# A graph, attention and mixture-of-experts block on one core: both layers' weight product moved to the front, the routing in 16-bit floats, the gates carried in the gathered rows

## The chip, the core and the metric

The kernel runs on one core of a Trainium2 chip. The metric is the device time of one execution in microseconds (us); a lower time is better. The profile is one execution taken with the hardware profiler; its times are counted from the first instruction, and its span from the first to the last.

The engines are named as in the profile: PE is TensorE's matmul, PEld its weight load, DVE is VectorE, ACT is ScalarE, POOL is GpSimd, SP is SyncE, which computes nothing and issues DMAs. Every engine takes its instructions in the order of the program; L405 is line 405 of the kernel. ACT and POOL can issue DMAs too.

## The reference

All data is 32-bit float. There are N = 1250 nodes with D = 768 features and 41,250 edges given as lists `src` and `dst` sorted by `dst`.

```python
xn = layernorm(x)
# graph part: two layers of attention over the edges, heads 4 x 192, then 2 x 96
h    = (layernorm(xn) * g + b) @ W1
e    = leaky_relu(s_src[src] + s_dst[dst])        # s = (h * a).sum(-1) per head
out1 = segment_sum(softmax over dst(e) * h[src], dst) + b1
out2 = the same with W2, a_src2, a_dst2, b2 on out1
gnn  = concat([xn, out2]) @ Wu + bu
# linear attention: q, k = elu(xn @ W + b) + 1, 12 heads of 64
mix  = (q @ (k.T @ v)) / (q @ k.sum) @ Wo + bo
x    = x + gnn + mix
# mixture of experts: 8 experts of 768 -> 384 -> 768, the best 2 for each node
xl   = layernorm(x); gate = xl @ Wg + bg
x    = x + sum over the best 2 experts e of gate[e] * (gelu(xl @ fW1[e] + fb1[e]) @ fW2[e] + fb2[e])
```

## The kernel before

Nodes are worked on in ten tiles of 125 (`NT = 10`). A tile framework takes the Python program, gives every instruction a place on its engine by priorities and its own model of durations, and sets the semaphores. So an instruction may stand far from its line's neighbours; the order on each engine is fixed when the program is built.

**Counting.** Edges are turned into a dense matrix of counts `AT` (125 partitions x 10 x 1250). A short start loads the edge lists, sorts out keys, and tests in a branch (L240) whether the slow general way is needed; it isn't for this data. Then `chunk` runs 41 times: two one-hot compares on DVE (`l_hot`, `k_hot`, L335), eight matmuls (`ec`, L350) and four additions into `AT` on DVE (L356). Between the chunks of each tile stands `features(t)`: the layer norm of a tile (L307 to L311) and six transposes (L319) with their copies (L321) into `xnT`.

**The weight product.** `weights()` folds layer 2 into layer 1. It makes the columns `W2e` from `W2` and the attention vectors (a product L381 and a reduction L383 for each of the two vectors), transposes `W1` in 48 matmuls (L394, copies L396), multiplies it with `W2e` (L405), scales the result into `Wg1` (L410), and makes two constant rows (L398, L417, L420, copied by L422 and L423). In the program it stands after tile 1. `gathered(t)` (L430) then multiplies each tile by `Wg1`; the framework puts these matmuls between the later chunks. When the memory of `weights()` is free, the loads of `Wk` and `Wv` (L453 to L455) follow on SP's queue.

After the last chunk the mask is made (L461 transposed by L465), and six heads of attention run (L504 to L569), with the k and v projections (L607) between them.

**Mix and routing.** For each tile: the q projection (L751), the sum over all parts (L781, L792), a layer norm, the row `xl` written to a table in HBM (`xl_d`, L802), the gate (L807, L810), and the routing. The routing ranks the eight gates (L817 to L826), counts places with two small matmuls (`pp`, L830), splits each place into a slot and a row, and writes two values into `inv`, the node's number and its gate, by matmuls of one-hots (`hot`, `put`, L849 to L854). All of it is in 32-bit floats. After the last tile `idx` (node of every place) and `gs` (gate of every place) are read out of `inv`.

**Experts.** Each expert has three fixed groups of 128 places. `gather(e)` fetches three groups of rows by indirect DMAs on POOL's queue (`xg`, L909; three buffers), and transposes them (L912). `hidden` and `give` are the two layers (L926, L938). `give` adds the bias, multiplies by the gate (L942), and adds the result to the output by an indirect, accumulating DMA on POOL's queue (L943). The program's order is

```python
xT = gather([r for r, _ in fixed(0)])
for e in range(NE):
    hT = hidden(ring[e], xT, FIX, fb1T[:, :, e:e + 1])
    if e + 1 < NE:
        xT = gather([r for r, _ in fixed(e + 1)])
    for j, (rows, gates) in enumerate(fixed(e)):
        give(ring[e], hT, j, rows, gates)
    if e + 4 < NE:
        ring.append(expert(fW1[e + 4], fW2[e + 4], fb2[e + 4]))
```

`expert` loads weights (L656 and L658, 1.15 MB each, and the bias L661) into a ring of four. Accumulating DMAs into the output wait for each other. After the eight experts, `other` treats one more group whose expert is known at run time only, and further ones under branches that this data doesn't take.

Of the kernel before, what the change touches and what calls it, by code (L numbers as in the profile page):

```python
# [38 lines left out]
N, D = 1250, 768  # L39
# [30 lines left out]
def gps_block(ctx: ExitStack, tc: tile.TileContext, x, src, dst, norm_g, norm_b, W1, a_src1, a_dst1,  # L70
# [60 lines left out]
    xl_d = dram.tile([N + 128, D], F32)  # L131
# [18 lines left out]
    def load_tile(t):  # L150
        xts[t] = ln.tile([PT, D], F32, name="xt", bufs=2)
        for p, tt in token_rows(t):
            nc.sync.dma_start(xts[t][p], xr[p, tt])

    load_tile(0)
# [4 lines left out]
    nb_row = fl.tile([96, D], F32)  # L160
    nc.sync.dma_start(W1_sb, W1.rearrange("(c p) f -> p c f", p=128))
# [6 lines left out]
    for t, a in zip(a2, (a_src2, a_dst2)):  # L168
        nc.sync.dma_start(t.rearrange("p h c -> p (h c)"), row_bcast(a, 96))
    nc.sync.dma_start(nb_row, row_bcast(norm_b, 96))  # L170

    rows = fl.tile([KC, 128], F32)
    colv = const.tile([128, KC], F32)
    nc.sync.dma_start(rows, norm_g.rearrange("(c p) -> c p", p=128))
    rows96 = fl.tile([26, 96], F32)
    col96 = const.tile([96, 26], F32)
    nc.sync.dma_start(rows96[0:8], b1.rearrange("(c p) -> c p", p=96))
    nc.sync.dma_start(rows96[8:10], b2.rearrange("(c p) -> c p", p=96))
    for k, a in enumerate((a_src1, a_dst1)):
        nc.sync.dma_start(rows96[10 + 8 * k:18 + 8 * k], a.rearrange("h (c p) -> (h c) p", p=96))  # L180
# [145 lines left out]
    with tc.tile_pool(name="ma_p", bufs=2, space=PSUM) as ma_p:  # L326
# [44 lines left out]
        def weights():  # L371
# [6 lines left out]
            for k in range(2):  # L378
                pr = fw.tile([96, 2, D], F32, name="W1T", bufs=2).rearrange(
                    "p a (i h c) -> p (a i) h c", h=H2, c=C2)  # L380
                nc.vector.tensor_mul(pr, heads2, a2[k][:, None].to_broadcast([96, 8, H2, C2]))  # L381
                at = 2 * (C2 + 1) + 2 * k
                nc.vector.tensor_reduce(W2e[:, :, at:at + 2], pr, AX.X, ALU.add)  # L383
# [54 lines left out]
        with tc.tile_pool(name="hot", bufs=2) as hot, \  # L438
                tc.tile_pool(name="ec_p", bufs=2, space=PSUM) as ec_p:
            for t in range(NT):  # L440
                for i in range(t * NC // NT, (t + 1) * NC // NT):
                    chunk(i, hot, ec_p)
                features(t)
                if t == 1:
                    weights()
                    setup.close()
                    kp = kps.enter_context(tc.tile_pool(name="kp", bufs=1, side="right"))
                    Wk_sb = kp.tile([128, KC, D], F32)
                    Wv_sb = kp.tile([128, KC, D], F32)
# [236 lines left out]
    zero = fp.tile([128, D], F32)  # L686
    nc.gpsimd.memset(zero, 0.0)
    nc.sync.dma_start(xl_d[N:], zero)
    nc.sync.dma_start(out[N:], zero)
# [4 lines left out]
    gs = fp.tile([128, NV + 1], F32)  # L694
# [4 lines left out]
    with ExitStack() as rs:  # L699
# [7 lines left out]
        def numbers(shape, pattern, base, mult, name):  # L707
            t = rp.tile(shape, F32, name=name)
# [8 lines left out]
        row128 = numbers([PT, 128], [[1, 128]], 0, 0, "row128")  # L717
        steps = numbers([128, NE, NJ - FIX], [[0, NE], [128, NJ - FIX]], 128 * FIX, 0, "steps")
        slot_row = numbers([PT, NV], [[1, NV]], 0, 0, "slot_row")
# [13 lines left out]
        nc.gpsimd.memset(gs[:, NV:], 0.0)  # L733
# [34 lines left out]
        for t in range(NT):  # L768
# [30 lines left out]
            xl = rl.tile([PT, D], F32, name="xl")  # L799
            normalise(xl, xt)  # L800
            for p, tt in token_rows(t):
                nc.sync.dma_start(xlr[p, tt], xl[p])  # L802
# [20 lines left out]
            sel = rl.tile([PT, NE], F32, name="sel")  # L823
# [13 lines left out]
            both = rl.tile([PT, 2, 2], F32, name="both")  # L837
            nc.vector.tensor_reduce(both, two, AX.X, ALU.add)
            b_i = rl.tile([PT, 2], I32, name="b_i")
            nc.vector.tensor_copy(b_i, both[:, 0])  # L840
# [6 lines left out]
            for k in range(2):  # L847
                hot = rl.tile([PT, 128], F32, name="hot")
                nc.vector.tensor_scalar(hot, row128, s_f[:, 1, k:k + 1], None, op0=ALU.is_equal)  # L849
                put = rl.tile([PT, 2, NV], F32, name="put")  # L850
                for i, v in enumerate((node1[:, t:t + 1], both[:, 1, k:k + 1])):
                    nc.vector.tensor_scalar(put[:, i], slot_row, s_f[:, 0, k:k + 1], v,
                                            op0=ALU.is_equal, op1=ALU.mult)
                nc.tensor.matmul(inv.rearrange("p a s -> p (a s)"), hot,  # L854
                                 put.rearrange("p a s -> p (a s)"), start=k == 0 and t == 0,
                                 stop=k == 1 and t == NT - 1)
        free = rp.tile([128, NV], F32)
        nc.vector.tensor_scalar(free, inv[:, 0], 0.0, nobody, op0=ALU.is_equal, op1=ALU.mult)
        nc.vector.scalar_tensor_tensor(idx[:, :NV], inv[:, 0], -1.0, free, op0=ALU.add,
                                       op1=ALU.add)  # L860
        nc.vector.tensor_copy(gs[:, :NV], inv[:, 1])
# [42 lines left out]
    def gather(rows):  # L904

        xT = sp.tile([128, KC, FIX * 128], F32, name="xsT")
        for j, r in enumerate(rows):
            xg = sp.tile([128, D], F32, name="xg", bufs=3)
            nc.gpsimd.indirect_dma_start(xg, None, xl_d, bass.IndirectOffsetOnAxis(r, 0))  # L909
            px = x_p.tile([128, 2, 512], F32, name="px")  # L910
            for c in range(KC):
                nc.tensor.transpose(px[:, c // 3, (c % 3) * 128:(c % 3 + 1) * 128],  # L912
                                    xg[:, c * 128:(c + 1) * 128], ident)
# [3 lines left out]
        return xT  # L917

    def hidden(w, xT, n, bias):
# [11 lines left out]
    def give(w, hT, j, rows, gates):  # L931
# [9 lines left out]
        nc.vector.tensor_add(halves(ys), py[:, :, :384], halves(wb))  # L941
        nc.scalar.mul(ys, ys, gates)  # L942
# [3 lines left out]
    def fixed(e):  # L946
        return [(idx[:, v:v + 1], gs[:, v:v + 1]) for v in range(e * NJ, e * NJ + FIX)]

    xT = gather([r for r, _ in fixed(0)])
    for e in range(NE):  # L950
        hT = hidden(ring[e], xT, FIX, fb1T[:, :, e:e + 1])
        if e + 1 < NE:
            xT = gather([r for r, _ in fixed(e + 1)])
        for j, (rows, gates) in enumerate(fixed(e)):
            give(ring[e], hT, j, rows, gates)
        if e + 4 < NE:
            ring.append(expert(fW1[e + 4], fW2[e + 4], fb2[e + 4]))

    def other(k):
# [7 lines left out]
        gates = sp.tile([128, 1], F32, name="gates")  # L967
        nc.vector.tensor_copy(gates, gs[:, bass.ds(ve, 1)])
# [4 lines left out]
        hT = hidden(w, gather([rows]), 1, bias)  # L973
        give(w, hT, 0, rows, gates)
# [41 lines left out]
```

## Time and profile before

| | us |
|---|---|
| median of 3 runs | 1179.41 (1175.86 to 1180.65) |
| the profiled execution | 1180.66 |
| its span | 1178.6 |
| PE busy | 1077.8 (91%) |
| DVE busy | 669.1 (57%) |
| ACT busy | 358.1 (30%) |
| POOL busy | 76.3 (6%) |

The profiled execution spends 2.1 us outside its span and stands 1.25 us above the median. Stages, by the first and last instructions of their lines: the start to 20.3, counting with the weight product to 193, the mask to about 212, attention to 594, loads and the k/v product to 622, mix and routing to about 937, experts to the end. A busy PE says only that matmuls are in its pipe; where it is the engine that others wait for must be read from the chain of waits and the timeline.

### The profile page before, as it was taken

How to read it: one execution, taken by the hardware profiler on the slowest of the kernel's cores; microseconds unless marked ns; L12 is line 12 of the kernel's file. 1: busy time of each engine (PE TensorE's matmuls, PEld its weight loads, DVE VectorE, ACT ScalarE, POOL GpSimd, SP SyncE). 2: the span in 40 equal slices, each digit the busy share in tenths (PEclk: the TensorE clock that was granted, in tenths of full speed). 3: DMA queues.
4: the chain of work that ended last, by engine and by line, in shares of the span. 5: the costliest groups of instructions: out<-in, count | busy, mean ns of one | idle time of the engine just before them, and what ended most of it. 6: DMA issues, size and time to landing. Idle time of an engine off the chain costs nothing.

```text
span 1178.6 us, 12106 instructions
## 1 busy us (share of the span) xinstructions
PE 1077.8 (91%) x4583; PEld 723.6 (61%) x4583; DVE 669.1 (57%) x1366; ACT 358.1 (30%) x527; POOL 76.3 (6%) x100
## 2 busy tenths in 40 slices
PE   2599998999999999988989999999999589999993
PEld 2586655578788878544545666666666356666652
DVE  6866666669696966687922555555555422222210
ACT  2131114373737373373712211111111011111111
POOL 1000000000000000000000000000000122322321
PEclk9999998999999999989989999999999789999997
DMA  5014000000000001000083111111123537777533
GB/s 156 27 51 163 16 25 1 1 1 1 1 1 1 1 1 53 1 0 1 1 319 103 40 40 40 40 40 40 39 65 106 191 91 188 200 209 219 121 56 54
DMA packets 33282, 79.62 MB, mean 68 GB/s; under 512 B 5258, under 2 KB 13020, under 8 KB 33208
## 3 DMA queue, kind: packets, MB, share of 16 engines
q1 hardware_dynamic: 27608, 59.02, 15.2%
q0 software_dynamic: 5600, 19.66, 8.4%
q8 instruction: 40, 0.66, 0.2%
q14 instruction: 34, 0.28, 0.1%
HBM read 60.37 MB, written 18.30 MB: 67 GB/s over the span
## 4 chain that ended last, share of the span: by engine, by line
PE 70%; DVE 20%; DMA 5%; issue 2%; ACT 2%; POOL 1%; DVEq 0%; SPq 0%; POOLq 0%; ACTq 0%
PE po L781 13%; PE ph L926 8%; PE py L938 7%; PE mm L430 7%; PE mm L607 7%; PE mm L751 7%; DVE scr L515 6%; DVE w L535 5%; DVE w L536 5%; PE ag L548 3%; PE ag L569 2%; PE u L792 2%; PE px L912 2%; PE mm L405 2%; DMA w<-in_L_gnn_Wu_dram 2%
## 5 line engine op out<-in xcount | busy, mean ns | idle before, releaser
L548 PE MATMUL ag<-kept,w 125*125 125x198 f32 x800 | 137.4, 333 | 5.1 <-DVE w L536 4.9
L548 PEld LDWEIGHTS ag<-kept,w 125*125 125x125 f32 x800 | 133.5, 188 | 9.0 <-DVE w L536 9.0
L926 PE MATMUL ph<-xsT,w 128*128 128x384 f32 (+1 forms) x324 | 100.6, 470 | 1.8 <-DVE xsT L915 1.8
L938 PE MATMUL py<-w,hT 128*128 128x384 f32 x300 | 100.6, 486 | 0.0
L430 PE MATMUL mm<-Wg,xnT 128*125 128x400 f32 x240 | 91.8, 520 | 1.0 <-DVE xnT L321 0.6
L607 PE MATMUL mm<-Wv_sb,xnT 128*125 128x384 f32 x240 | 85.7, 489 | 4.8 <-DVE kvacc L627 4.8
L535 DVE TENSOR_TENSOR w<-v,w 125x1250 f32<-125x1250 f32 x60 | 86.3, 1453 | 6.6 <-ACT w L533 5.9
L515 DVE CUSTOM_DVE_ANT_0 scr<-ss_row,mask 125x1250 bf16<-125x1250 f32 x60 | 87.2, 1453 | 0.5 <-ACT ss_row L506 0.2
L781 PE MATMUL po<-w,xnT 128*125 128x384 f32 x240 | 84.8, 496 | 2.6 <-DMA w<-in_L_gnn_Wu_dram 2.6
L536 DVE SCALAR_TENSOR_TENSOR w<-w,AT 125x1250 f32<-125x1250 f32 x60 | 86.4, 1455 | 0.4
L926 PEld LDWEIGHTS ph<-xsT,w 128*128 128x128 f32 x324 | 59.8, 193 | 41.4 <-DVE xsT L915 2.4
L607 PE MATMUL mm<-Wk_sb,xnT 128*125 128x384 f32 x240 | 84.4, 486 | 0.0
L534 ACT ACTIVATE v<-dn_row,sl 125x1250 f32<-125x1250 f32 x60 | 79.3, 1333 | 16.9 <-DVE w L535 16.4
L751 PE MATMUL mm<-w,xnT 128*125 128x384 f32 x240 | 84.2, 489 | 0.0
L915 DVE COPY xsT<-px 128x384 f32<-128x384 f32 x50 | 25.5, 552 | 99.2 <-PE px L912 77.3
L781 PE MATMUL po<-w,qT 128*125 128x384 f32 x240 | 80.8, 486 | 0.0
L938 PEld LDWEIGHTS py<-w,hT 128*128 128x128 f32 x300 | 55.3, 190 | 33.9
L941 DVE TENSOR_TENSOR ys<-py,wb 128x768 f32<-128x768 f32 x25 | 23.9, 958 | 74.0 <-PE py L938 45.5
L781 PEld LDWEIGHTS po<-w,xnT 128*125 128x125 f32 x240 | 44.2, 190 | 30.1 <-DMA w<-in_L_gnn_Wu_dram 2.8
L781 PEld LDWEIGHTS po<-w,qT 128*125 128x125 f32 x240 | 44.2, 188 | 29.4
L607 PEld LDWEIGHTS mm<-Wv_sb,xnT 128*125 128x125 f32 x240 | 42.4, 187 | 31.1 <-DVE kvacc L627 6.9
L751 PEld LDWEIGHTS mm<-w,xnT 128*125 128x125 f32 x240 | 43.6, 188 | 27.6 <-ACT qT L321 0.2
(274 smaller groups left out, 1415.6 us busy)
## 6 DMA issues: line engine op xcount, KB each, us to landing
w<-in_L_ffn_W_dram SPq DMA_DIRECT2D x18, 1152.0 KB
xt<-in_x_dram SPq DMA_DIRECT2D x20, 336.0 KB
wb<-in_L_ffn_b_dram SPq DMA_DIRECT2D x9, 384.0 KB
out_dram<-xt SPq DMA_DIRECT2D x10, 336.0 KB
xl_d<-xl SPq DMA_DIRECT2D x10, 336.0 KB
W_sb<-in_L_gnn_W_dram SPq DMA_DIRECT2D x1, 2304.0 KB
Wk_sb<-in_L_mix_Wk_dram SPq DMA_DIRECT2D x1, 2304.0 KB
Wv_sb<-in_L_mix_Wv_dram SPq DMA_DIRECT2D x1, 2304.0 KB
```

Source lines behind the costliest of these rows:

```text
L430: nc.tensor.matmul(ps[:PT, :2 * (CG + 2)], xnT[:, c, t * PT:(t + 1) * PT], Wg1[:, c, 2 * k:2 * k + 2].rearrange("p h c -> p (h c)"), start ...
L515: nc.vector.tensor_tensor_reduce(scr, ss_row, mask[:, t], 1.0, 0.0, ALU.mult, ALU.max, top[:, t:t + 1])
L534: nc.scalar.activation(v, dn_row, AF.Exp, bias=sl[:, st:st + 1])
L535: nc.vector.tensor_tensor(w, v, w, op=ALU.max)
L536: nc.vector.scalar_tensor_tensor(w, w, 2.0, AT[:, st, :N], op0=ALU.min, op1=ALU.mult)
L548: nc.tensor.matmul(ag[:, t // 2, o:o + CG], w[:, t * PT:(t + 1) * PT], gw[:, st, hd], start=st == 0 and t % 2 == 0, stop=st == NT - 1, ski ...
L607: nc.tensor.matmul(ps[:PT, :384], xnT[:, c, t * PT:(t + 1) * PT], w[:, c, half], start=c == 0, stop=c == KC - 1)
L751: nc.tensor.matmul(ps[:PT, :384], xnT[:, c, tk], Wq_sb[:, c, half], start=c == 0, stop=c == KC - 1)
L781: nc.tensor.matmul(po[k][:, :384], l, r[:, k * 384:(k + 1) * 384], start=i == 0, stop=i == len(parts) - 1)
L915: nc.vector.tensor_copy(xT[:, 3 * a:3 * a + 3, j * 128:(j + 1) * 128], px[:, a, :384].rearrange("p (b n) -> p b n", b=3))
L926: nc.tensor.matmul(ph[:, :n * 128], w[0][:, o:o + 128], xT[:, c, :n * 128], start=c == 0, stop=c == KC - 1)
L938: nc.tensor.matmul(py[:, k, :384], hT[:, f, j * 128:(j + 1) * 128], w[:, o:o + 384], start=f == 0, stop=f == FC - 1)
```

## The change

`weights()` is called before the first tile's chunks. Its eight small loads are issued by ACT instead of SP and stand ahead of the others in the program; the first tile of `x` is loaded after `W1` and `W2`. `pr` gets memory of its own. The loads of `Wk` and `Wv` stand after tile 2 instead of tile 4.

In the routing, `row128`, `slot_row`, `ones`, `tri`, `cum`, `sel`, `hot` and `put` become 16-bit floats, and `inv` holds only the node's number. The gate leaves the routing: it is written into eight further columns of the row table `xl_d` (776 columns instead of 768), comes back with the gathered row `xg`, and `give` reads it there. So `xg` is kept until its `give` is done, and has six buffers instead of three. `hidden` is renamed `inner`.

```diff
-    xl_d = dram.tile([N + 128, D], F32)
+    xl_d = dram.tile([N + 128, D + NE], F32)
...
-    load_tile(0)
     W1_sb = fl.tile([128, KC, D], F32)
...
+    nc.scalar.dma_start(rows, norm_g.rearrange("(c p) -> c p", p=128))
...
+    nc.scalar.dma_start(rows96[0:8], b1.rearrange("(c p) -> c p", p=96))
+    nc.scalar.dma_start(rows96[8:10], b2.rearrange("(c p) -> c p", p=96))
+    for k, a in enumerate((a_src1, a_dst1)):
+        nc.scalar.dma_start(rows96[10 + 8 * k:18 + 8 * k], a.rearrange("h (c p) -> (h c) p", p=96))
     nc.sync.dma_start(W1_sb, W1.rearrange("(c p) f -> p c f", p=128))
...
     for t, a in zip(a2, (a_src2, a_dst2)):
-        nc.sync.dma_start(t.rearrange("p h c -> p (h c)"), row_bcast(a, 96))
-    nc.sync.dma_start(nb_row, row_bcast(norm_b, 96))
...
+        nc.scalar.dma_start(t.rearrange("p h c -> p (h c)"), row_bcast(a, 96))
+    nc.scalar.dma_start(nb_row, row_bcast(norm_b, 96))
+    load_tile(0)
     load_tile(1)
...
-                pr = fw.tile([96, 2, D], F32, name="W1T", bufs=2).rearrange(
+                pr = fw.tile([96, 2, D], F32, name="pr").rearrange(
...
+            weights()
             for t in range(NT):
                 for i in range(t * NC // NT, (t + 1) * NC // NT):
                     chunk(i, hot, ec_p)
                 features(t)
-                if t == 1:
-                    weights()
+                if t == 0:
                     setup.close()
...
-                if t == 4:
+                if t == 2:
                     nc.sync.dma_start(Wk_sb, Wk.rearrange("(c p) f -> p c f", p=128))
...
-        ones = rp.tile([PT, 128], F32)
+        ones = rp.tile([PT, 128], F16)
-        tri = rp.tile([PT, 128], F32)
+        tri = rp.tile([PT, 128], F16)
-        cum = rp.tile([PT, NT + 1, NE], F32)
+        cum = rp.tile([PT, NT + 1, NE], F16)
-        inv = g_p.tile([128, 2, NV], F32, name="inv", bufs=1)
+        inv = g_p.tile([128, NV], F32, name="inv", bufs=1)
...
-            xl = rl.tile([PT, D], F32, name="xl")
-            normalise(xl, xt)
+            xl = rl.tile([PT, D + NE], F32, name="xl")
+            normalise(xl[:, :D], xt)
...
-            gate = rl.tile([PT, NE], F32, name="gate")
+            gate = xl[:, D:]
             nc.vector.tensor_add(gate, pg[:PT, :NE], bg_b)
+            for p, tt in token_rows(t):
+                nc.sync.dma_start(xlr[p, tt, D:], gate[p])
...
-            two = rl.tile([PT, 2, 2, NE], F32, name="two")
-            for i, a in enumerate((at, gate)):
-                nc.vector.tensor_mul(two[:, i], kth, a[:, None, :].to_broadcast([PT, 2, NE]))
+            two = rl.tile([PT, 2, NE], F32, name="two")
+            nc.vector.tensor_mul(two, kth, at[:, None, :].to_broadcast([PT, 2, NE]))
...
-                hot = rl.tile([PT, 128], F32, name="hot")
+                hot = rl.tile([PT, 128], F16, name="hot")
                 nc.vector.tensor_scalar(hot, row128, s_f[:, 1, k:k + 1], None, op0=ALU.is_equal)
-                put = rl.tile([PT, 2, NV], F32, name="put")
-                for i, v in enumerate((node1[:, t:t + 1], both[:, 1, k:k + 1])):
-                    nc.vector.tensor_scalar(put[:, i], slot_row, s_f[:, 0, k:k + 1], v,
-                                            op0=ALU.is_equal, op1=ALU.mult)
-                nc.tensor.matmul(inv.rearrange("p a s -> p (a s)"), hot,
-                                 put.rearrange("p a s -> p (a s)"), start=k == 0 and t == 0,
+                put = rl.tile([PT, NV], F16, name="put")
+                nc.vector.tensor_scalar(put, slot_row, s_f[:, 0, k:k + 1], node1[:, t:t + 1],
+                                        op0=ALU.is_equal, op1=ALU.mult)
+                nc.tensor.matmul(inv, hot, put, start=k == 0 and t == 0,
                                  stop=k == 1 and t == NT - 1)
...
-        nc.vector.tensor_copy(gs[:, :NV], inv[:, 1])
...
-            xg = sp.tile([128, D], F32, name="xg", bufs=3)
+            xg = sp.tile([128, D + NE], F32, name="xg", bufs=6)
...
+        if isinstance(e, int):
+            gates = xg[:, D + e:D + e + 1]
+        else:
+            gates = sp.tile([128, 1], F32, name="gates")
+            nc.vector.tensor_copy(gates, xg[:, bass.ds(e + D, 1)])
         nc.scalar.mul(ys, ys, gates)
...
-    xT = gather([r for r, _ in fixed(0)])
+    nxt = gather(fixed(0))
     for e in range(NE):
-        hT = hidden(ring[e], xT, FIX, fb1T[:, :, e:e + 1])
+        xT, xgs = nxt
+        hT = inner(ring[e], xT, FIX, fb1T[:, :, e:e + 1])
         if e + 1 < NE:
-            xT = gather([r for r, _ in fixed(e + 1)])
-        for j, (rows, gates) in enumerate(fixed(e)):
-            give(ring[e], hT, j, rows, gates)
+            nxt = gather(fixed(e + 1))
+        for j, rows in enumerate(fixed(e)):
+            give(ring[e], hT, j, rows, xgs[j], e)
```

More of the change, by code (lines that the diff above doesn't have):

```diff
@@ L160, in gps_block @@
     nb_row = fl.tile([96, D], F32)
+    rows = fl.tile([KC, 128], F32)
+    colv = const.tile([128, KC], F32)
+    nc.scalar.dma_start(rows, norm_g.rearrange("(c p) -> c p", p=128))
+    rows96 = fl.tile([26, 96], F32)
+    col96 = const.tile([96, 26], F32)
+    nc.scalar.dma_start(rows96[0:8], b1.rearrange("(c p) -> c p", p=96))
+    nc.scalar.dma_start(rows96[8:10], b2.rearrange("(c p) -> c p", p=96))
+    for k, a in enumerate((a_src1, a_dst1)):
+        nc.scalar.dma_start(rows96[10 + 8 * k:18 + 8 * k], a.rearrange("h (c p) -> (h c) p", p=96))
     nc.sync.dma_start(W1_sb, W1.rearrange("(c p) f -> p c f", p=128))
@@ L168, in gps_block @@
     for t, a in zip(a2, (a_src2, a_dst2)):
-        nc.sync.dma_start(t.rearrange("p h c -> p (h c)"), row_bcast(a, 96))
-    nc.sync.dma_start(nb_row, row_bcast(norm_b, 96))
[L172 to L180, printed above, removed]
+        nc.scalar.dma_start(t.rearrange("p h c -> p (h c)"), row_bcast(a, 96))
+    nc.scalar.dma_start(nb_row, row_bcast(norm_b, 96))
+    load_tile(0)
     load_tile(1)
@@ L684, in gps_block @@
             nc.scalar.copy(Wo_sb[:, c, half], ps[:, :384])
-    zero = fp.tile([128, D], F32)
+    zero = fp.tile([128, D + NE], F32)
     nc.gpsimd.memset(zero, 0.0)
     nc.sync.dma_start(xl_d[N:], zero)
-    nc.sync.dma_start(out[N:], zero)
+    nc.sync.dma_start(out[N:], zero[:, :D])
     ring = [expert(fW1[0], fW2[0], fb2[0])]
@@ L693, in gps_block @@
     idx = fp.tile([128, NV + 1], I32)
-    gs = fp.tile([128, NV + 1], F32)
     fb1T = fp.tile([128, FC, NE], F32)
@@ L705, in gps_block, with numbers @@
         u_p = rs.enter_context(tc.tile_pool(name="u_p", bufs=2, space=PSUM))
-        def numbers(shape, pattern, base, mult, name):
-            t = rp.tile(shape, F32, name=name)
+        def numbers(shape, pattern, base, mult, name, dt=F32):
+            t = rp.tile(shape, dt, name=name)
             nc.gpsimd.iota(t, pattern=pattern, base=base, channel_multiplier=mult,
@@ L716, in gps_block @@
         nc.vector.tensor_scalar(upto, upto, 0.0, None, op0=ALU.is_ge)
-        row128 = numbers([PT, 128], [[1, 128]], 0, 0, "row128")
+        row128 = numbers([PT, 128], [[1, 128]], 0, 0, "row128", F16)
         steps = numbers([128, NE, NJ - FIX], [[0, NE], [128, NJ - FIX]], 128 * FIX, 0, "steps")
-        slot_row = numbers([PT, NV], [[1, NV]], 0, 0, "slot_row")
+        slot_row = numbers([PT, NV], [[1, NV]], 0, 0, "slot_row", F16)
         base = numbers([PT, NE], [[128 * NJ, NE]], -1, 0, "base")
@@ L732, in gps_block @@
         nc.vector.tensor_scalar(idx[:, NV:], nobody, -1.0, None, op0=ALU.add)
-        nc.gpsimd.memset(gs[:, NV:], 0.0)
         for f in range(FC):
@@ L797, in gps_block @@
                 nc.sync.dma_start(outr[p, tt], xt[p])
-            xl = rl.tile([PT, D], F32, name="xl")
-            normalise(xl, xt)
+            xl = rl.tile([PT, D + NE], F32, name="xl")
+            normalise(xl[:, :D], xt)
             for p, tt in token_rows(t):
-                nc.sync.dma_start(xlr[p, tt], xl[p])
+                nc.sync.dma_start(xlr[p, tt, :D], xl[p, :D])
             xT = rl.tile([128, KC, PT], F32, name="xT")
@@ L822, in gps_block @@
             kth = rl.tile([PT, 2, NE], F32, name="kth")
-            sel = rl.tile([PT, NE], F32, name="sel")
+            sel = rl.tile([PT, NE], F16, name="sel")
             for k in range(2):
@@ L833, in gps_block @@
             nc.vector.tensor_add(at, pp[:PT, :NE], base)
-            two = rl.tile([PT, 2, 2, NE], F32, name="two")
-            for i, a in enumerate((at, gate)):
-                nc.vector.tensor_mul(two[:, i], kth, a[:, None, :].to_broadcast([PT, 2, NE]))
-            both = rl.tile([PT, 2, 2], F32, name="both")
+            two = rl.tile([PT, 2, NE], F32, name="two")
+            nc.vector.tensor_mul(two, kth, at[:, None, :].to_broadcast([PT, 2, NE]))
+            both = rl.tile([PT, 2], F32, name="both")
             nc.vector.tensor_reduce(both, two, AX.X, ALU.add)
             b_i = rl.tile([PT, 2], I32, name="b_i")
-            nc.vector.tensor_copy(b_i, both[:, 0])
+            nc.vector.tensor_copy(b_i, both)
             s_i = rl.tile([PT, 2, 2], I32, name="s_i")
@@ L847, in gps_block @@
             for k in range(2):
-                hot = rl.tile([PT, 128], F32, name="hot")
+                hot = rl.tile([PT, 128], F16, name="hot")
                 nc.vector.tensor_scalar(hot, row128, s_f[:, 1, k:k + 1], None, op0=ALU.is_equal)
-                put = rl.tile([PT, 2, NV], F32, name="put")
-                for i, v in enumerate((node1[:, t:t + 1], both[:, 1, k:k + 1])):
-                    nc.vector.tensor_scalar(put[:, i], slot_row, s_f[:, 0, k:k + 1], v,
-                                            op0=ALU.is_equal, op1=ALU.mult)
-                nc.tensor.matmul(inv.rearrange("p a s -> p (a s)"), hot,
-                                 put.rearrange("p a s -> p (a s)"), start=k == 0 and t == 0,
+                put = rl.tile([PT, NV], F16, name="put")
+                nc.vector.tensor_scalar(put, slot_row, s_f[:, 0, k:k + 1], node1[:, t:t + 1],
+                                        op0=ALU.is_equal, op1=ALU.mult)
+                nc.tensor.matmul(inv, hot, put, start=k == 0 and t == 0,
                                  stop=k == 1 and t == NT - 1)
         free = rp.tile([128, NV], F32)
-        nc.vector.tensor_scalar(free, inv[:, 0], 0.0, nobody, op0=ALU.is_equal, op1=ALU.mult)
-        nc.vector.scalar_tensor_tensor(idx[:, :NV], inv[:, 0], -1.0, free, op0=ALU.add,
-                                       op1=ALU.add)
-        nc.vector.tensor_copy(gs[:, :NV], inv[:, 1])
+        nc.vector.tensor_scalar(free, inv, 0.0, nobody, op0=ALU.is_equal, op1=ALU.mult)
+        nc.vector.scalar_tensor_tensor(idx[:, :NV], inv, -1.0, free, op0=ALU.add, op1=ALU.add)
         for e in range(1, 4):
@@ L906, in gather @@
         xT = sp.tile([128, KC, FIX * 128], F32, name="xsT")
+        xgs = []
         for j, r in enumerate(rows):
-            xg = sp.tile([128, D], F32, name="xg", bufs=3)
+            xg = sp.tile([128, D + NE], F32, name="xg", bufs=6)
             nc.gpsimd.indirect_dma_start(xg, None, xl_d, bass.IndirectOffsetOnAxis(r, 0))
@@ L916, in gather, with inner @@
                                       px[:, a, :384].rearrange("p (b n) -> p b n", b=3))
-        return xT
-    def hidden(w, xT, n, bias):
+            xgs.append(xg)
+        return xT, xgs
+    def inner(w, xT, n, bias):
         hT = sp.tile([128, FC, FIX * 128], F32, name="hT")
@@ L929, in hidden, with give @@
         return hT
-    def give(w, hT, j, rows, gates):
+    def give(w, hT, j, rows, xg, e):
         w, wb = w
@@ L946, in fixed @@
     def fixed(e):
-        return [(idx[:, v:v + 1], gs[:, v:v + 1]) for v in range(e * NJ, e * NJ + FIX)]
-    xT = gather([r for r, _ in fixed(0)])
+        return [idx[:, v:v + 1] for v in range(e * NJ, e * NJ + FIX)]
+    nxt = gather(fixed(0))
     for e in range(NE):
-        hT = hidden(ring[e], xT, FIX, fb1T[:, :, e:e + 1])
+        xT, xgs = nxt
+        hT = inner(ring[e], xT, FIX, fb1T[:, :, e:e + 1])
         if e + 1 < NE:
-            xT = gather([r for r, _ in fixed(e + 1)])
-        for j, (rows, gates) in enumerate(fixed(e)):
-            give(ring[e], hT, j, rows, gates)
+            nxt = gather(fixed(e + 1))
+        for j, rows in enumerate(fixed(e)):
+            give(ring[e], hT, j, rows, xgs[j], e)
         if e + 4 < NE:
@@ L966, in other @@
         nc.vector.tensor_copy(rows, idx[:, bass.ds(ve, 1)])
-        gates = sp.tile([128, 1], F32, name="gates")
-        nc.vector.tensor_copy(gates, gs[:, bass.ds(ve, 1)])
         bias = sp.tile([128, FC, 1], F32, name="bias")
@@ L972, in other @@
                    fW2[bass.ds(ee, 1)].rearrange("o d f -> (o d) f"), fb2[bass.ds(ee, 1)])
-        hT = hidden(w, gather([rows]), 1, bias)
-        give(w, hT, 0, rows, gates)
+        xT, xgs = gather([rows])
+        hT = inner(w, xT, 1, bias)
+        give(w, hT, 0, rows, xgs[0], ee)
     def others(k):
```

## The prediction

> **What bounds the kernel now.** I read the page's chain by engine first, then windows by stage, the chain in order of time around the edited lines, and POOL's timeline in the experts. The chain:
>
> ```profile
> PE 70%; DVE 20%; DMA 5%; issue 2%; ACT 2%; POOL 1%; DVEq 0%; SPq 0%; POOLq 0%; ACTq 0%
> ```
>
> PE carries most of it, but by stages. In the windows (stretch, length, busy time of PE, PEld, DVE, ACT, POOL):
>
> ```profile
> 20.30:51.00 30.70, 14.35 (x91) 12.29 (x91) 27.70 (x70) 4.39 (x11) 0.20 (x1) 1.00 0.14 40
> 51.00:83.60 32.60, 32.28 (x198) 30.73 (x199) 19.73 (x53) 14.36 (x38) 0.00 (x0) 0.95 0.05 13
> 83.60:193.00 109.40, 102.52 (x511) 63.97 (x510) 79.47 (x234) 18.48 (x52) 1.49 (x13) 0.98 0.19 65
> 622.00:916.00 294.00, 293.98 (x1096) 180.27 (x1095) 150.29 (x405) 54.47 (x87) 0.00 (x0) 1.00 0.18 54
> ```
>
> The reader sees a stretch bound by DVE (27.7 of 30.7), one in which PE makes the weight product with DVE 40% idle, then counting with PE ahead, and a mix and routing stage in which PE never rests: there every PE microsecond counts in full. The steps the change touches, in the chain:
>
> ```profile
> 50.98 6.57 PE mm L405 x24
> 79.11 4.47 PE mm L420 x16
> 851.97 0.35 PE g L830 x4
> 854.99 0.67 PE inv L854 x4
> ```
>
> In the experts PE repeats with a period of 25.31 (start of the last transposes of one expert to that of the next, 1017.64, 1042.95, 1068.27). POOL in one such period:
>
> ```profile
> 1018.63 0.94 POOL L909 DMA_INDIRECT xg<-xl_d,idx  x1 [1.03 <-PE px L912]
> 1021.95 1.62 POOL L943 DMA_INDIRECT out_dram<-ys,idx  x1 [2.37 <-ACT ys L942]
> 1028.70 1.59 POOL L943 DMA_INDIRECT out_dram<-ys,idx  x1 [5.13 <-DMA out_dram<-ys,idx]
> 1040.59 1.56 POOL L943 DMA_INDIRECT out_dram<-ys,idx  x1 [10.30 <-DMA out_dram<-ys,idx]
> 1042.46 1.02 POOL L909 DMA_INDIRECT xg<-xl_d,idx  x1 [0.30 <-issue]
> ```
>
> The third scatter of an expert waits 10.30 for the second to land, while the next expert's weights load, and the gathers stand behind it. They do no harm now, because they are gathers for an expert further ahead.
>
> **Counting and the weight product.** In the order of the changed program the product comes first; the five key operations (1.9 by their rows) and the first norm move behind the branch. DVE, idle from 15.94 to 20.34 at the branch, then starts on the product at about 21: two L381 (1.72), two L383 (1.73), two copies `by` (0.95), one one-hot (0.6), 9.4 in all, and some 0.6 of waits. The first L405 starts at ~31 instead of 50.98; from there to the end of L420 it took 32.6, so the product ends at ~63.6 instead of 83.6: 20 earlier. `W1` and `W2` are the first large loads, and the DMA share of 0.91 between 7.8 and 20.3 shows them done by about then.
>
> Nearly all of the 20 is paid back. At 83.6 the kernel before has counted 12 of 41 chunks and turned two tiles; after the product the changed one has counted four and turned none. Left on PE: 292 L350 at 0.0588, 17.2; 58 L319 at 0.107, 6.2; 216 passes L430 at 0.335, 72.4; 24 L607 at 0.323, 7.7: 103.5. Left on DVE: 146 additions into `AT` at 0.22, 32; 70 one-hots at 0.58, 40.6; eight tiles' norms and copies at 3.0, 25; small ones 3: 100.6. In the kernel before the same sums were 98.7 and 80.3, and took 109.4: DVE has lost its slack. Cutting the new PE order at the transposes and taking the larger engine in each of the nine pieces gives 112.5. The same cutting gives 100.2 for before, 9.2 too little; the misfit is 1.1 over the four tiles where PE leads clearly and 2.7 each over the three where both are near even. Five tiles are near even now: 13.5 and 1, so 127, and counting ends at 190.6 instead of 193.2. Gain **2.6**; without any misfit 17; with 22 (2.7 for eight tiles) a loss of 5. I take the middle value because the trace shows the misfit in just such tiles. From the mask on the orders are the same up to the routing, so the shift passes through; the wait of 18.4 for `Wu` at 594 follows the stage's memory and moves with it.
>
> The small loads on ACT's queue: SP's unblocked issues cost 0.23 to 0.43, so eight cost 2 to 3.5, and ACT sits idle from 4.80 to 7.85: hidden. If one blocks as SP's at 7.80 did (4.83), up to 4.5 of ACT lies open, ahead of the copies that the product's first matmuls need. I take 0. The loads of `Wk` and `Wv` were issued at 83.67 and landed near 99; they now start at about 64, first use near 94: hidden, else some 5. `x`'s tile 4 queues behind them and lands in time.
>
> **Mix and routing.** Per tile `pp` (four passes) takes 0.35 and `inv` 0.67. In 16 bits each matmul is one pass; the nearest row is the 16-bit `ec`, eight in 0.47 in a stream, one alone 0.22. I take 0.12 for each pair, so 0.78 less per tile, 7.0 over nine tiles. In the last tile the chain is latency: one `put` of two (0.47), `inv` (1.57), the product with the gate (0.08), the copy `gs` (0.15), some 2.3 together. Gain **9.3**, bounds 2.3 (a 16-bit pass no shorter) and 9.5.
>
> The gate writes add two SP issues per tile, 0.76, about 3 after `xl`'s. Behind them on SP stands the next tile's load of `x`: issued at ~850.3 instead of 847.13, it lands 2 to 3 later, and L783 needs it at 855.85: hidden, else ~1 a tile, 9. The last gate is known at 928.8 and written near 932; the first gather starts at 937.47 behind PE's last matmuls: hidden, else a few. Expert 3's W2 moves from 925.56 to ~929.7, needed after 1000: hidden. The Trainium skill ("DMA: Bandwidth & Descriptors", "Specifications") says that writes under 512 B become read-modify-writes. The gate's rows are 32 B, and no run shown has the price.
>
> **Experts.** With six `xg` buffers freed only by `give`, POOL's order changes from nine gathers ahead, then three scatters and three gathers, to six gathers ahead, then one scatter, one gather in turn. The gather whose data PE needs 25.31 after the last transposes now stands behind the third scatter. That scatter starts, for experts 0 to 4, 22.1, 21.1, 22.95, 22.1 and 21.6 after those transposes (1040.59 less 1017.64 is the third), and 18.9 for expert 5, beside which no weights load. From scatter to gather's issue is 1.87 (1040.59 to 1042.46), and a gather alone took 4.06 from issue to use (the chain's 937.47). The data come 5.93 after the scatter's start, so PE stalls 2.7, 1.7, 3.6, 2.75, 2.2 and 0: 13.0 in six experts. That is the low end. If the gather's data go only after the scatter's land on the one queue (the scatter of 1021.95 frees its buffer at 1028.03: 6.0) and 0.4 MB then take 1.3 at the 319 GB/s of the page's fastest slice, 7.3 stands for 5.93: 20.7. Two gathers in between also delay the second scatter by about 0.7 per expert: 24. I take **18**, between the ends, as the rows show scatters serialised but no gather directly behind one. Below 0 is excluded: the period is PE's own work, and the change takes none of it away.
>
> The skill's rule ("DMA: Bandwidth & Descriptors", "Two DMAs through the same engine are not ordered") has descriptors of one queue started in order but pipelined, reading and writing apart. By it the low end would hold, and the sum would be 5 lower. The rows of the scatters show 6.0 from start to buffer free because each waits for the one before by a semaphore, which tells nothing against the rule.
>
> **Sum.** −2.6 − 9.3 + 18 = +6.1. On the profiled execution (1180.66; span 1178.6 and 2.1 outside): 1186.8; it stands 1.25 above the median of the runs shown, so **1186** by the median. About 0.5% (5.9) is what a measurement of this kernel can tell from no change.
>
> **Rivals.**
> Counting pays off in full. For it: PE and DVE alternate in short pieces, and the misfit may come from PE's order alone. Against: 2.7 in each even tile. Gain 17, so −17 − 9.3 + 18: **1171**. It decides when the stage ends before ~184.5.
> No stalls in the experts. For it: nine buffers' worth of slack is only spent down to six; the gather may land sooner under other traffic. Against: 5.93 exceeds the distance of 2.4 to 4.2 left. −2.6 − 9.3: **1167.5**. It decides where the stall per expert is below about 2.
> DVE takes the counting over, on the slower side: every tile has the misfit (+5), the routing's matmuls save half as much (−4.7), the gathers go serial (+20.7), +21 in all: **1200**. It decides when the stage ends after 198.
> The change doesn't do what it says: the product comes first in the order, but a blocked issue on ACT or a late `W1` starts L405 at 40 and not 31. DVE and PE then have chunks to fill with only four ahead; 5 to 7 of it is lost, near **1192**, inside the forecast's range.
>
> **How the numbers follow.** Forecast, with the late product in it, 0.58 (1178 to 1193: slower 0.38, same 0.20); counting in full 0.20 (faster 0.14, same 0.06); no stalls 0.08 (faster); DVE-bound 0.14 (slower). That is faster 0.22, same 0.26, slower 0.52. The range takes the low case in to 1169 and the high one to 1201; the ends of single costs beyond these make up the rest.
>
> **What would show it.** Right: first L405 near 31, L420 done near 64; the stage ends at 190 ± 4, DVE above 90% busy in it; L854 near 0.1 to 0.2 a pair; POOL alternates L946 and L906; the transposes wait for a DMA into `xg` 2 to 5 in five experts, period 28 to 29.5 in place of 25.31, and expert 5's is unchanged. Wrong: a counting end below 184 or above 198; a period that stays at 25.3; L854 as long as before; or L783 waiting for `x` in every tile.

## The result, and the profile after

The changed kernel takes 1190.42 us (median of 6 runs, 1187.24 to 1192.49) against 1179.53 for the kernel before (6 runs): a ratio of 1.0096, 95% interval 1.0072 to 1.012. It is 10.9 slower. The forecast was 1186 with a range of 1169 to 1201 and slower as its likeliest side.

The profiled execution has a span of 1188.4, 9.8 more than before. By stages (first use in the trace, before and after): counting ends at 193.2 and 190.1; the first `po` (the mix's sum over all parts) starts at 613.0 and 607.5; the experts' first transposes start at 941.6 and 925.4, 16.2 earlier; and from there to the end it takes 237.0 and 263.0. So the change gains 16 up to the experts and loses 26 in them.

The windows that answer to those of before, in the same columns, for the start of the product, the product, the counting, and the mix with the routing:

```profile
20.30:34.70 14.40, 3.44 (x14) 2.42 (x14) 11.09 (x15) 2.04 (x6) 0.39 (x1) 0.86 0.02 5
34.70:67.40 32.70, 32.55 (x198) 31.08 (x199) 19.31 (x53) 16.23 (x41) 0.00 (x0) 0.87 0.08 24
67.40:190.10 122.70, 108.41 (x588) 69.06 (x587) 99.63 (x295) 19.78 (x54) 1.48 (x13) 1.00 0.18 61
622.00:916.00 294.00, 289.56 (x1075) 176.18 (x1075) 151.10 (x395) 51.48 (x82) 0.00 (x0) 0.99 0.18 58
```

The product is 16 earlier, and the counting behind it takes 122.7 where before it took 109.4. PE's timeline around the other edited steps (start, length):

```profile
34.75 5.67 PE L405 MATMUL mm<-W2e,W1T 96*128 96x200 f32 x16 [7.45 <-issue]
...
840.39 0.17 PE L831 MATMUL g<-sel,tri 125*128 125x8 f16 x1
840.42 0.17 PE L831 MATMUL g<-cum,ones 125*128 125x8 f16 x1
...
842.46 0.20 PE L853 MATMUL inv<-put,hot 125*128 125x80 f16 x1
```

In 16 bits the two passes of `pp` start 0.03 apart, and each of them or of `inv` takes no more than 0.04 from the pipe. The experts are where the reader should look longest. POOL over one expert, with what its waits ended on:

```profile
1015.86 1.59 POOL L946 DMA_INDIRECT out_dram<-ys,idx  x1 [8.59 <-ACT ys L945]
1017.75 0.99 POOL L906 DMA_INDIRECT xg<-xl_d,idx  x1 [0.31 <-PE py L936]
1022.38 1.59 POOL L946 DMA_INDIRECT out_dram<-ys,idx  x1 [3.64 <-DMA out_dram<-ys,idx]
1024.27 0.99 POOL L906 DMA_INDIRECT xg<-xl_d,idx  x1 [0.30 <-issue]
1033.87 1.59 POOL L946 DMA_INDIRECT out_dram<-ys,idx  x1 [8.61 <-ACT hT L926]
1035.76 0.98 POOL L906 DMA_INDIRECT xg<-xl_d,idx  x1 [0.31 <-PE px L909]
```

Scatter and gather take turns; the gather of 1035.76 stands behind a scatter that waited 8.61 (the profile names ACT, which had long been done; it is the scatter of 1022.38 that has to land). PE waits for exactly these rows:

```profile
1032.74 0.82 PE L909 MATMUL px<-ident,xg 128*128 128x128 f32 x6
1033.40 1.46 PE L936 MATMUL py<-w,hT 128*128 128x384 f32 x4
1034.72 0.84 PE L909 MATMUL px<-ident,xg 128*128 128x128 f32 x6
...
1041.15 1.51 PE L909 MATMUL px<-ident,xg 128*128 128x128 f32 x6 [4.29 <-DMA xg<-xl_d,idx]
1042.45 3.79 PE L936 MATMUL py<-w,hT 128*128 128x384 f32 x8
```

The second thing to see is the length of what follows. Six transposes take 1.51 where the group before took 0.84, and eight matmuls of `py` 3.79 where four had just taken 1.46. Windows around two such stalls; the third column from the right is the granted clock:

```profile
1007.60:1011.40 3.80, 1.44 (x6) 0.56 (x5) 1.02 (x2) 0.00 (x0) 0.00 (x0) 1.00 0.73 173
1011.40:1014.00 2.60, 2.58 (x12) 1.85 (x13) 1.37 (x3) 0.00 (x0) 0.00 (x0) 1.00 0.00 0
...
1036.80:1041.10 4.30, 0.06 (x1) 0.00 (x0) 0.00 (x0) 0.00 (x0) 0.00 (x0) 1.00 0.67 162
1041.10:1044.00 2.90, 2.85 (x9) 2.27 (x10) 1.02 (x2) 0.00 (x0) 0.00 (x0) 0.51 0.00 0
1044.00:1047.00 3.00, 3.00 (x9) 1.68 (x9) 0.96 (x1) 0.93 (x1) 0.00 (x0) 0.91 0.00 0
```

After a stall of 2.38 (ending at 1011.42) the clock stays at 1.00; after the one of 4.29 PE works at about half speed for 3 us. The five stalls are 3.84, 2.38, 4.29, 4.08 and 3.42, together 18.0. The periods in which they lie, from one expert's first transposes to the next's, are 32.12, 27.83, 31.40, 30.95 and 30.51; over 25.31 that is 26.3. So 8.3 of the loss is not waiting. Nearly all of that is slow matmuls behind the waits: from the start of the third group to the next expert's first transposes it takes 24.16, 21.32, 22.99, 22.75 and 22.97, where an undisturbed expert takes 21.32, and that is 7.6 more.

### The profile page after: what moved, and what is told of

Its sections match the earlier page's. It is cut to its first block, busy times and chain, and to the rows that moved or that the text cites. A ratio compares the mean times of both kernels' runs of the same rounds, so it can differ in the third digit from the quotient of the medians.

```text
span 1188.4 us, 12023 instructions
## 1 busy us (share of the span) xinstructions
PE 1068.1 (90%) x4542; PEld 712.1 (60%) x4542; DVE 663.1 (56%) x1335; ACT 358.3 (30%) x527; POOL 76.8 (6%) x99
## 5 line engine op out<-in xcount | busy, mean ns | idle before, releaser
L936 PE MATMUL py<-w,hT 128*128 128x384 f32 x300 | 105.6, 505 | 0.0
L515 DVE CUSTOM_DVE_ANT_0 scr<-ss_row,mask 125x1250 bf16<-125x1250 f32 x60 | 87.3, 1455 | 0.5 <-ACT ss_row L506 0.2
L936 PEld LDWEIGHTS py<-w,hT 128*128 128x128 f32 x300 | 58.2, 200 | 36.5 <-issue 4.7
L945 ACT ACTIVATE ys<-ys,xg 128x768 f32<-128x768 f32 x24 | 22.4, 935 | 126.0 <-DVE ys L939 116.4
```

The lines of the kernel that those rows point to most:

```text
L515: nc.vector.tensor_tensor_reduce(scr, ss_row, mask[:, t], 1.0, 0.0, ALU.mult, ALU.max, top[:, t:t + 1])
L936: nc.tensor.matmul(py[:, k, :384], hT[:, f, j * 128:(j + 1) * 128], w[:, o:o + 384], start=f == 0, stop=f == FC - 1)
```

## The experiments

The theory after the result: row buffers that live until the gate is used put each expert's third gather behind a scatter (18 of waiting), and four of five such waits also halve PE's clock for some microseconds (8). The rivals: the longer rows or the shared queue as such; slow matmuls from another cause; a larger gain of the moved product, hidden by other parts.

**Early copy of the gates (e1_early), and the same again (e1_again).** From the changed kernel:

```diff
-            xg = sp.tile([128, D + NE], F32, name="xg", bufs=6)
+            xg = sp.tile([128, D + NE], F32, name="xg", bufs=3)
...
-            xgs.append(xg)
+            gx = sp.tile([128, NE], F32, name="gx", bufs=6)
+            nc.vector.tensor_copy(gx, xg[:, D:])
+            xgs.append(gx)
```

> The changed kernel, but the eight gate columns of a gathered row are copied to a small tile on DVE right after the transposes' copies, so that a row buffer is free once it is transposed, and three row buffers are enough again. GpSimd's order is then that of the kernel before: nine gathers ahead, then three scatters and three gathers in turn. Theory (the time went into the third gather of each expert, which stands behind a scatter because row buffers live until the gate is used): the period in the experts returns to 25.3 us, all of the 26 us between the first transposes and the end come back, and the time is 1164 (1161 to 1167). Rival (the longer rows or more traffic on the queue make the gathers late, whatever their order): the transposes still wait 2 to 4 us per expert, and the time stays above 1180.

Measured 1163.42; ratio to before 0.9878 (0.9853 to 0.9902). The only waits left in the experts are the three at their start; every later period is 25.31, with the same 776-column rows and the same queue. One expert's groups and the next expert's first, with nothing to wait for:

```profile
999.63 0.82 PE L909 MATMUL px<-ident,xg 128*128 128x128 f32 x6
1001.61 0.85 PE L909 MATMUL px<-ident,xg 128*128 128x128 f32 x6
1003.62 0.84 PE L909 MATMUL px<-ident,xg 128*128 128x128 f32 x6
1024.95 0.82 PE L909 MATMUL px<-ident,xg 128*128 128x128 f32 x6
```

The rival falls: the lifetime of the buffers cost the whole 26 to 27 (1190.42 less 1163.42 is 27.0; the two ratios to the kernel before give 25.7).

> The kernel with the early copy of the gates once more, beside the bridged one on the same chip: 1163, within the interval of its first runs (ratio 0.985 to 0.990).

Measured 1164.18, 0.989 (0.9872 to 0.9909).

**Seven row buffers (e5_seven).** The changed kernel with `bufs=7` for `xg`, nothing else.

> The changed kernel with seven row buffers in place of six, nothing else. One scatter and one gather still alternate on GpSimd, but the third gather of an expert now stands behind the second scatter of the expert two before it, not behind the third. Theory (what counts is which scatter the third gather stands behind): it is issued some 10 us earlier, no stall is left, 1164 to 1168. Rival (the alternation itself costs, because gathers and scatters share one queue and delay each other): the period falls from 31 to 28 at best, time 1175 to 1185.

Measured 1170.05, 0.9935 (0.9916 to 0.9954), 2 above the theory's end. All five waits are gone and the periods are 25.31, though scatters and gathers still alternate: it is not the alternation. But there is a new wait, once:

```profile
1106.43 1.06 PE L909 MATMUL px<-ident,xg 128*128 128x128 f32 x6 [3.13 <-issue]
```

```profile
1105.25 0.15 DVE L944 COPY gates<-xg 128x1 f32 x1 [14.46 <-DMA xg<-xl_d,rows]
1105.32 1.01 DVE L912 COPY xsT<-px 128x384 f32<-128x384 f32 x2
```

The first row is PE's, the other two DVE's. On DVE a small copy for the extra group waits for that group's rows, whose gather was issued behind a third scatter; the copies that free PE's bank stand behind it. From this last expert's first transposes (1101.19) to the extra group's it takes 41.8 instead of 36.9 in e1_early.

**Work in the gaps (e2_fill).** The changed kernel with 24 transposes, that nothing reads, ahead of the five third groups:

```diff
+            for _ in range(fill if j == 2 else 0):
+                nc.tensor.transpose(px[:, 1, 384:512], ident, ident)
```

> The changed kernel with 24 extra transposes of the identity into unused columns ahead of the third transposes of experts 2 to 6, some 2.7 us of PE work that nothing reads, in the place where PE waits for the gathered rows. Theory (8 of the 26 us lost in the experts are matmuls at a granted clock of 0.50 for some 5 us after each stall of over 3 us): the extra work lies in the stall, the clock stays at 1.0, the row of slow matmuls after the stalls goes, and the kernel gets faster by about 8, 1182. Rival A (the matmuls after a stall are slow for another reason, such as the traffic of weights and rows): no change, 1190. Rival B (PE reaches the extra work late, so that it lies on the path): slower, 1193 to 1203.

Measured 1182.81, 1.0042 (1.0026 to 1.0058): 7.6 less than the changed kernel (6.4 by the two ratios), by adding work. The waits that remain are 2.16, 0, 0.25, 0 and 0.41, and the five periods together exceed five times 25.31 by 19.0 instead of 26.3. Behind two of the filled gaps:

```profile
1014.00:1018.00 4.00, 3.96 (x21) 2.72 (x20) 1.98 (x3) 0.00 (x0) 0.00 (x0) 1.00 0.03 10
1043.20:1047.00 3.80, 3.78 (x16) 2.59 (x17) 1.98 (x3) 0.53 (x1) 0.00 (x0) 1.00 0.00 0
```

The clock is 1.00 in both, beside the same loads, so rival A falls. Not all of the gain is the clock's. From an expert's first transposes to its third group it takes 9.01, 6.89, 7.10, 6.85 and 7.25, in the changed kernel 7.96, 6.51, 8.41, 8.20 and 7.54: 1.5 less in all, since the rows came earlier in three of the five. From the third group to the next expert it takes 23.04 behind the wait of 2.16, which halved the clock again, and 21.35 or 21.36 behind the other four: 5.7 less than the changed kernel, of the 7.6 that the slow matmuls cost there.

**The product and its loads alone (e3_weights).** The kernel before with `weights()` ahead of the chunks, the small loads on ACT and the early `Wk` and `Wv`.

> The kernel before with the first part of the change alone: the weight product ahead of the counting, the small loads on ACT's queue, the loads of Wk and Wv after tile 2. Routing and experts are untouched. Theory (the 20 us that the product is earlier are paid back in the counting, since DVE has lost its slack there): counting ends about 3 us earlier than before, and the time is 1173 to 1177. Rival (the profile of the changed kernel understates it, and other parts hid a larger gain): counting ends at 175 to 180, time 1162 to 1166. Rival (the small differences of the stages are noise): 1179.

Measured 1176.21, 0.9983 (0.997 to 0.9995), so 2.0 less with 0.6 to 3.5 as the interval. In its profile the counting ends at 193.9, so not 3 earlier as the theory had it; what this profile gains lies behind the counting (see "Between the stages" below). The rival with 12 to 16 falls; that of noise is only just outside the interval.

**The routing alone, with the early copy (e4_routing).** The kernel before with the 16-bit routing and gates in the rows, three row buffers and `gx` as in e1_early.

> The kernel before with the routing's part of the change alone (16-bit floats, gates in the rows), with the gates copied out early and three row buffers; the weight product and its loads stay where they were. Theory (the routing saves some 10 us, from the passes of pp and inv and the shorter chain of the last tile, and the rest of the change neither helps nor hurts it): first transposes of the experts near 931 instead of 941.6, period 25.3, time 1167 (1165 to 1170). Rival (the gain up to the experts came mostly from the earlier weight product): 1173 to 1177.

Measured 1168.22, 0.9911 (0.9894 to 0.9928): 10.5 less than before. The first transposes are at 930.1. With e3's 2.0 that makes 12.5, near e1's 14.4 and 13.0.

**The rows alone (e6_rows).** The kernel before with gates in the rows and six row buffers; the routing stays in 32 bits.

> The kernel before with the gates in the rows and six row buffers alone: routing in 32-bit floats (inv is half as wide, since it holds no gate), weight product where it was. Theory (the loss in the experts belongs to this part alone and does not need the others): stalls of 2 to 4 us ahead of five third transposes, 26 us lost there, 3 to 4 us gained by the narrower inv, time 1200 (1197 to 1204). Rival (the stalls depend on PE arriving earlier than before): 1180 to 1188.

Measured 1200.00, 1.0176 (1.0159 to 1.0193). The waits are 0.74, 4.25, 2.75, 2.20, 3.60 and 3.25, and the experts take 260.4 instead of 237.0. This part alone makes the loss, with PE arriving as late as before. The 3 to 4 that I expected from the narrower `inv` did not show: the first transposes stand at 941.7, as before. So 1200 meets the theory partly by luck: 23.4 lost in the experts against 26, and nothing gained against 3 to 4.

**DVE relieved in the counting (e7_actcopy).** On e1_early, the copies of the transposed tiles move to ACT:

```diff
-            turn(xnT[:, :, t * PT:(t + 1) * PT], xn, ma_p, "tr", nc.vector.tensor_copy)
+            turn(xnT[:, :, t * PT:(t + 1) * PT], xn, ma_p, "tr", nc.scalar.copy)
```

> The kernel with the early copy of the gates (1163.4), and in the counting the copies of the transposed tiles moved from DVE to ACT: 18 of 0.54 us after the product. Theory (with the product ahead, DVE's chunks and PE's transposes hand over to each other in the counting, and DVE is what fails to keep up): counting ends 3 to 6 us earlier, time 1158 to 1161. Rival (PE bounds the counting also there, with 108 of 123 us busy): no change, 1163. Rival (the copies stand behind the scaling copies on ACT and make PE wait): 1165 to 1170.

Measured 1192.88, some 29 slower, and not for any of the reasons on record. Counting ends at 193.2, but the framework placed the k and v projections otherwise, and attention takes 355.8 from its first row to its last, instead of 325.2 (first to last L515). The run says nothing on whether DVE bounds the counting: its effect there is smaller than what the new order did elsewhere.

**Work at the experts' start (e9_start).** On e1_early, 16, 5 and 5 transposes of the identity ahead of the first three groups.

> The kernel with the early copy of the gates (1163.4), and 16, 5 and 5 extra transposes of the identity ahead of the first three groups of transposes in the experts, that nothing reads. Theory (the first transposes and the first 6 us of the first hidden layer run at a granted clock of 0.50 because PE had been mostly idle; extra work in PE's waits ends that earlier): first hidden layer 12 to 13 us instead of 14.8, time 1159 to 1161. Rival (the clock does not depend on work that is only filling, or the filling lies on the path): 1163 to 1166.

Measured 1163.57, 0.9878 (0.9857 to 0.99): nothing. The framework put the 16 far forward, and the fives could start only when DVE's copies were done, so waits of 1.21 stayed. The first hidden layer still takes 14.42, and the fives lie on the path: from the first transposes to the next expert's it is 24.0, in e1_again 22.1.

**Bridges over the gaps (e11_bridge).** On e1_early, in the program behind the first and the third group of transposes; the framework ran the second six ahead of the third group:

```diff
+            if bridge[j]:
+                spare = h_p.tile([128, 512], F32, name="ph")
+                for _ in range(bridge[j]):
+                    nc.tensor.transpose(spare[:, :128], xg[:, :128], ident)
```

> The kernel with the early copy of the gates (1163.4), and six extra transposes of rows that have landed already, into a spare bank, behind the first and before the third group of transposes, so that PE's two waits of 1.16 us there are bridged. Nothing reads them. Theory (the clock comes back only after some 5 us of work without gaps, and the filling in e9 left both gaps open): the clock is back some 4 us earlier than in the kernel without bridges, the first hidden layer takes 12 to 13 us instead of 14.7, and the time is 1160 to 1162. Rival (gaps of about 1 us do not matter): first hidden layer unchanged at 14.4 to 14.8, time 1163 to 1166.

Measured 1161.46, 0.9872 (0.9849 to 0.9894), beside 1164.18 for the kernel without bridges on the same chip. The intervals overlap, so a shorter time isn't shown; the shorter first hidden layer is, by the trace. Two rows of the bridged kernel, then one of e1_again:

```profile
928.00:930.00 2.00, 2.00 (x15) 1.63 (x13) 0.98 (x5) 0.00 (x0) 0.96 (x2) 0.77 0.02 6
930.00:932.00 2.00, 0.97 (x8) 0.64 (x6) 0.53 (x2) 0.00 (x0) 1.13 (x2) 1.00 0.70 208
```

```profile
933.78 14.77 PE L926 MATMUL ph<-xsT,w 128*128 128x384 f32 x36 [0.65 <-DVE xsT L912]
```

With bridges the clock is back before 930, though a wait of 0.55 is left ahead of the third group, and the first hidden layer takes 11.88 instead of 14.77; from the first transposes to the next expert's it is 19.1 instead of 22.1. Its median is the lowest here.

## Why the prediction was right or wrong

**The product's place.** L405 starts at 34.75, not 31. DVE left the branch at 23.27 (before: 20.34) and ran the key operations first, so that the product began at 25.44 where I had put 21; from there it took the 9 to 10 of the sum. Of these 4.4 about 1.9 are the key operations: I had put them behind the branch and left them out of the product's start. Why the branch is 2.9 later stays open; more bytes are moved ahead of it (4.56 MB by 23.2 against 4.16 by 20.3), and no run separated that. L420 then ends at 67.9 instead of 63.6. The small loads were hidden on ACT, as I had taken them: each issue took 0.28 to 0.56 and the last was done at 4.1. But I had misread ACT's row: its idle time before 7.85 is 4.80 long and doesn't begin at 4.80.

**Paid back in the counting.** 190.6 was predicted, 190.1 came, but partly by luck: the stage began 3.8 later than I thought (67.4 for 63.6) and took 122.7, not 127. Work left was close on DVE (99.6 against my 100.6) and higher on PE (108.4 against 103.5). The misfit term of 13.5 was too large, and DVE above 90% was wrong: it is at 81%. Nor is one profile a measure here. In eight profiles of kernels with the product first (e7, whose order is another, left out) the counting ends between 187.3 and 193.9 (mean 191.3), in three with the old place between 191.9 and 193.2 (mean 192.7). The means differ by 1.4, less than either group scatters. In time, e3's 2.0 is the measure, and my 2.6 lies in its interval; but its profile has that gain behind the counting, so the agreement is partly luck too. That the 20 are paid back is shown; that DVE's lost slack is the reason was argued from the sums and is not shown, since e7 failed to test it.

**Routing.** The period of the tiles falls from 29.53 to 28.77 (the first matmuls of L807 and L806), 0.76 against 0.78 predicted; from the last gate's matmuls to the first transposes it is 13.2 instead of 15.7, 2.5 against 2.3. e4 gives 10.5 for the part against 9.3, and in its profile the stretch from the first gate's matmuls to the experts is 9.5 shorter. The gate writes cost nothing that shows: `xt` waits for a DMA once, for the first tile and before any gate is written (8.4; before, 7.0). Whatever the read-modify-write of rows under 512 B (the Trainium skill, "DMA: Bandwidth & Descriptors", "Specifications") adds to them is not on the path here.

**Between the stages.** 3.5 of the 16.2 at the experts' start come from neither part, and the prediction, which let the shift pass through unchanged, has no term for them. They are not scatter. From the end of the counting to the first `po` the eight product-first profiles take 417.1 to 417.5, the three with the old place 419.1 to 420.2. 1.8 of it is in attention, where PE's order in e3 is that of the kernel before. The first row is the kernel before, the second e3:

```profile
500.00:516.00 16.00, 12.86 (x36) 6.37 (x36) 11.76 (x9) 12.15 (x14) 0.00 (x0) 0.79 0.00 0
500.00:516.00 16.00, 12.86 (x47) 6.77 (x47) 13.64 (x11) 14.51 (x17) 0.00 (x0) 1.00 0.00 0
```

All three profiles with the old place show 0.79 here, from 6.83 us at half clock (506.16 to 512.99 in the kernel before); none of the eight does. Two waits of PE, 1.4 and 1.75 long, stand ahead of that in both kernels. So this gain comes with the moved product, but through the clock and not through less work; how the clock decides is taken up below.

**The experts, the step that was mis-sized.** The order on POOL, the five experts, the spared sixth and the sum of the waits came as written: 18.0 against 18. The rows came 7.0 to 7.9 after the third scatter's start (1033.87 to 1041.15), nearer to my serial end of 7.3 than to 5.93. With 7.3 my own sum was 20.7, so that the middle, 18, was met is partly luck. The low end, which I had put beside the Trainium skill's rule on pipelined descriptors ("DMA: Bandwidth & Descriptors", "Two DMAs through the same engine are not ordered"), was too little here, though weight loads ran beside the gathers too, and no run parts the two. What failed is the price of a wait: I took a microsecond of waiting for a microsecond of time. Four of the five waits also halved the granted clock for 2.9 to 5.8 us of the work after them; that is nearly all of the 8.3 that make 26.3 out of 18. In the profiles the change costs 9.8 where the sum had 6.1: 8 more in the experts, less 3.5 between the stages and 0.8 in the counting and the routing.

The profile of before held the clue: its first hidden layer in the experts takes 13.93 behind a sparse stretch of PE, every later one 11.61. And the Trainium skill ("TensorE: Matmul & The Clock Gate", "What's actually happening") says that PE falls to half its clock after an idle window of about 3.4 us and returns after a busy one, the windows running freely. The waits of 3.42 to 4.29 agree; but the clock also fell after waits of 2.75 (e6) and 2.16 (e2), and not after 2.38 or 2.20 (e6).

The traces tell these apart. In all twelve the granted clock changes only on a grid of 3.41 us, fixed within the run. Cut along it, the wait of 2.38 (1009.04 to 1011.42) is split, that of 2.75 (1024.51 to 1027.26) is not. Two stretches of the changed kernel, then two of e6:

```profile
1007.00:1010.41 3.41, 2.04 (x11) 1.15 (x10) 1.02 (x2) 0.00 (x0) 0.27 (x1) 1.00 0.95 201
1010.41:1013.83 3.42, 2.41 (x12) 1.78 (x13) 1.20 (x3) 0.00 (x0) 0.00 (x0) 1.00 0.03 13
```

```profile
1024.75:1028.16 3.41, 0.90 (x7) 0.91 (x8) 0.02 (x1) 0.00 (x0) 0.00 (x0) 1.00 0.40 126
1028.16:1031.57 3.41, 3.41 (x7) 1.70 (x6) 1.96 (x3) 0.00 (x0) 0.00 (x0) 0.50 0.02 5
```

PE idles 1.37 and 1.01 in the first two and 2.51 in the third, behind which the clock is 0.50 for a whole stretch although PE is at work again. The others fit: 2.16 lies nearly whole in one stretch of e2, 2.20 is cut into 1.07 and 1.13, and of the two waits in attention 2.02 fall into one stretch of the kernel before, but 1.56 and 1.58 into two of e3. In these traces no stretch at full clock with more than 1.81 of idle PE was followed by another at full clock. Falls behind less idle time occur too, so this is a reading of the traces and not the whole rule, and no run moved a wait along the grid on purpose.

**The rivals.** "Counting in full" is refuted by e3, "no stalls" by the waits, "DVE takes over" by the end at 190.1. The late product came about half way: L405 at 34.75, between 31 and 40, by the branch and the key operations and not by ACT.

## What to carry to other kernels

A buffer that one more reader holds longer changes the order of a queue: see behind which scatter each gather now stands, and copy out the few bytes that the late reader needs. Price a wait on PE by what follows it too: here 18 us of waits cost 26. A gain of 20 us at one point of a stage is worth what the rest of the stage leaves of it, here about 2.

## What the runs showed of the hardware

Adding 24 idle transposes in front of each of five waits made a kernel 7.6 us faster (1190.42 to 1182.81), for the most part since PE's clock then stayed at 1.00. The clock changed on a grid of 3.41 us: a wait of 2.75 inside one stretch of it halved the clock, one of 2.38 that was cut by a step did not. At the experts' start, with waits of 1.16 between pieces of 1.51, the clock was back 13.4 us after the first transposes (e1_again); with these waits bridged it was back after 3.3 (e11_bridge). A gather behind an accumulating scatter on GpSimd's queue, with weight loads beside it, brought its rows to their use 5.1 to 6.0 us after its issue; a gather alone took 4.06.
